# Layer two of a two-layer graph attention kernel: later rounds for some stages, and one wait for the row gathers of a round

## The chip, the cores and the metric

The kernel runs on one core of a Trainium2 chip. The metric is the device time of one execution in microseconds (us); lower is better. The kernel before takes 2671.73 us, the median of three runs (2668.62 to 2673.74).

Five engines of the core matter here. TensorE (PE) multiplies matrices and transposes tiles; its weight loads are listed apart (PEld). VectorE (DVE) and ScalarE (ACT) do elementwise work and reductions. GpSimd (POOL) does little here but issue indirect transfers, which fetch rows of a table by an index for each partition. SyncE (SP) issues the plain transfers. Each engine goes through its instructions in order; between engines they wait for each other by semaphores. The DMA engines carry out the transfers.

## The reference, cut to what matters

Two graph convolutions with attention, over 6250 nodes and 106,250 edges (50,000 in both directions and a loop at each node), the edges sorted by destination. There are 128 features in two heads of 64; an edge has 64 given attributes and 32 cosines of a time difference.

```python
def _transformer_conv(h, edge_attr, src, dst, Wq, bq, Wk, bk, Wv, bv, We, Ws, bs):
    q = (h @ Wq + bq).reshape(n, H, C)
    k = (h @ Wk + bk).reshape(n, H, C)
    v = (h @ Wv + bv).reshape(n, H, C)
    e = (edge_attr @ We).reshape(-1, H, C)
    alpha = einsum('ehc,ehc->eh', q[dst], k[src] + e) / sqrt(C)
    ex = exp(alpha - segment_max(alpha, dst)[dst])
    a = ex / segment_sum(ex, dst)[dst]
    out = segment_sum((v[src] + e) * a[:, :, None], dst)
    return out.reshape(n, H * C) + h @ Ws + bs

rel_t_enc = cos((node_vec[src] - edge_weight)[:, None] * time_w + time_b)
edge_attr = concatenate([rel_t_enc, edge_attr_64], axis=-1)
h = _transformer_conv(x, edge_attr, src, dst, ...)        # layer one
h = relu((h - mean(h, 0)) / sqrt(var(h, 0) + 1e-5) * bn_g + bn_b)
h = _transformer_conv(h, edge_attr, src, dst, ...)        # layer two
return layernorm(x + h)
```

## The kernel before

**Tiling.** The edges are cut into NC = 104 chunks of 1024 (`CE`), eight tiles (`T`) of 128 edges each. As the edges are sorted by destination, a chunk touches a window of at most NN = 64 nodes, which is handled as NQ = 4 groups of 16 nodes; each group takes part in three edge tiles (`window`, L693), one of them possibly from the chunk before. Both layers run through `conv(c, ...)` (L740), layer one with c = 0 and layer two with c = 1, one round for each chunk and some more for the pipeline. Layer two takes about the second half of the span, from some 1400 us on. No scheduler reorders the instructions (`tc.manual_schedule()`): each engine gets them in the order in which the program writes them, and waits are put in where data ask for them.

**What happens to a chunk in layer two**, with the tiles that the profile names:

- `fetch` (L768), SyncE: loads the edge attributes into the feature tile `ff`, the tables of the window (`ftab`, one transfer for each group), the cosines of layer one (`fz`), the turned attributes (`fet`), and the residual rows (`fr`).
- `gather` (L810), GpSimd: eight indirect transfers (L815), each of 128 rows of the hidden features, from `hn_d` to `ff`. They are issued three rounds ahead of the scores (`lead`, L824).
- `turn_in` (L876), TensorE: two times four transposes of the gathered rows into `fpx` (L885); ScalarE copies them to `fft` (L889).
- `score` (L900), TensorE: about 20 matmuls of the tables with `fft` and `fet` into `fps` (L916).
- `lowest` (L921), VectorE: the row minimum of the scores (L924) and a limit (L926); `weigh` (L928), ScalarE: the exponential (L931) into `fs`.
- `turn_weights` (L933), TensorE: three transposes of `fs` (L940) into `fppt`; ScalarE copies them to `fpt` (L941).
- `gather_sums` (L944), TensorE: 24 matmuls (L956) of `fpt` with `ff`, which sum weighted rows, attributes and weights for each node and head into the PSUM tile `fpa`.
- `divide` (L960), VectorE: divides these sums by the sums of weights (L963 to L966) into `fa`, and makes a 0/1 matrix `fsel` (L968).
- `finish_turn` (L976), TensorE: two joins (L978, L979; two instructions each in the profile), matmuls with `fsel` that turn `fa` and put its rows in place; VectorE copies the result to `fat` (L981).
- `product` (L984), TensorE: the closing products with the value weights and the edge weights (L993, L994, eight instructions in the profile) into PSUM.
- `complete` (L1000): VectorE adds the residual rows and takes away the mean (L1032 to L1034), ScalarE squares (L1036); for every second chunk come a square root with its table load (L1039), a reload of the table of the exponential (L1042) and a reciprocal. `store` (L1047), ScalarE: scales the rows; SyncE writes them out a little later (`send`).
- `attributes` (L1141 in the loop): VectorE copies the cosines `fz` into `ff`.

**The round loop** (L1059 to L1149) handles in round k chunk k+3 (fetched and gathered), k+1 (turned in), k (scores, lowest, weigh), k-1 (turned weights, sums), k-2 (divide, joins) and k-3 (products, complete). The order on TensorE is: scores of k, products of k-3, turned weights of k-1, joins of k-2, first half of the turning in of k+1, second half, extra work, sums of k-1. The extra work (`hide`, `pull`) is, in the first rounds, the writing of normalised rows to `hn_d`, and later up to four matmuls of the layer's tables (`tables`, L625) at a time, with some of the residual.

**Holds of GpSimd.** `bring` (L1068) issues the gathers one by one and ties each to a step of TensorE in the same round, so that they keep pace with it: the first to the end of the previous round's sums (`ended`), the second to the fourth score group (`half`), the third to the turned weights, the fourth to the joins, the fifth and sixth to the two halves of the turning in, the seventh and eighth to the fourth and the eighth of the 24 sums. Such a tie (`tc.add_manual_dep`, L819) is a wait on GpSimd.

**Buffers.** PSUM has eight banks: four for `fpx`, `fppt` and the extra work (`p_tr`), two for the scores (`p_s`), two for `fpa` (`p_a`). A bank of `p_a` belongs to one chunk: its first half holds the sums (`s.pa`), its second half the joins (`s.po`), and the products go into the place of the first join. In SBUF layer two has six feature tiles `ff` (L744: `bufs=6 if c else AHEAD + 3`, with AHEAD = 4) and seven of `fr` (L806).

**The last rounds.** `SWITCH` is NC - 3 = 101. From there on `finish` (product and complete) of k-2 takes the place of product and complete of k-3, and behind the loop the last chunks are written out stage by stage (L1148 to L1189). For the first RAW = 6 chunks the rows come from layer one's raw output `h_d`, and `normalise` (L970) is applied to them on VectorE.

Of the kernel before, what the change touches and what calls it, by code (L numbers as in the profile page):

```python
# [10 lines left out]
OP = mybir.AluOpType  # L11
# [53 lines left out]
SWITCH = NC - 3  # L65
STARTS = (*range(0, NC - 2, LG), NC - 2, NC - 1)
# [599 lines left out]
def ordered(ctx: ExitStack, tc: tile.TileContext, pl, x, dst, edge_attr_64, conv2, bn_g, bn_b, out):  # L666
# [73 lines left out]
    def conv(c, extra, first_blocks=None):  # L740
# [27 lines left out]
        def fetch(k):  # L768
# [9 lines left out]
            s.f = f = load.tile([P, T, FW], F32, name="ff")  # L778
# [22 lines left out]
            if c:  # L801
# [4 lines left out]
                s.r = load.tile([NN, D], F32, name="fr", bufs=7)  # L806
# [137 lines left out]
        def gather_sums(k):  # L944
# [3 lines left out]
            s.po = bank[:, 1].rearrange("p (i n) -> p i n", i=2)  # L948
# [35 lines left out]
        def product(k):  # L984
            po, at = ch[k].po, ch[k].at
            if c == 0:
                nc.tensor.matmul(po[:, 0], wv[c], at[:, 0], start=True, stop=False)
                nc.tensor.matmul(po[:, 0], web[c], at[:, 1], start=False, stop=True)
                return
            at = at.rearrange("p i (n h) -> p i n h", h=H)  # L990
            for h in range(H):
                r = slice(h * C, (h + 1) * C)
                nc.tensor.matmul(po[:NN, 0, r], at[:, 0, :, h], wv[c][:, r], start=True, stop=False)  # L993
                nc.tensor.matmul(po[:NN, 0, r], at[:, 1, :, h], web[c][:, r], start=False, stop=True)  # L994
# [5 lines left out]
        def complete(k):  # L1000
            s = ch.pop(k)
            po = s.po
            if c == 0:

                res = small.tile([P, NN], F32, name="fres")
                heads = po[:, 0].rearrange("p (n h) -> p n h", h=H)
# [25 lines left out]
            nc.vector.scalar_tensor_tensor(res, po[:NN, 0], 1.0, s.r, op0=OP.mult, op1=OP.add, accum_out=mean)  # L1032
# [25 lines left out]

        with cs, tc.manual_schedule():  # L1059
            ended = None  # L1060
            for k in range(-lead(-NC), NC - 2 if c else NC + 3):
                def on(j):
                    return 0 <= j < NC

# [25 lines left out]
                if on(k - 3) and k <= SWITCH:  # L1090
                    product(k - 3)
# [11 lines left out]
                if on(k - 3) and k <= SWITCH:  # L1103
# [30 lines left out]
                if on(k - 2) and k >= SWITCH:  # L1134
# [3 lines left out]
                if c and on(k):  # L1138
                    if k < RAW:
                        normalise(k)  # L1140
                    nc.vector.tensor_copy(ch[k].f[:, :, 1 + D:1 + D + TD], ch[k].z)  # L1141
# [6 lines left out]
            if c:  # L1148
                last = NC - 1  # L1149

                def attributes(k):
                    nc.vector.tensor_copy(ch[k].f[:, :, 1 + D:1 + D + TD], ch[k].z)
# [407 lines left out]
```

## Time and profile before

| | before |
|---|---|
| median of 3 runs | 2671.73 us |
| profiled execution, own time | 2670.95 us |
| its span | 2669.1 us |
| mean granted TensorE clock | 0.879 |
| HBM traffic over the span | 141 GB/s |
| stretch 1460 to 2580 us (layer two): PE busy | 785.88 us of 1120 |
| the same: DVE, ACT, POOL busy | 331.08, 398.83, 698.15 us |
| the same: clock, DMA share | 0.87, 0.56 |

All times in the profile are of one execution. A line of the timeline has the start in us, the duration in us, the engine, the line of the program, the operation, the written and read tiles with their shapes, and the count of equal instructions that were drawn together; in square brackets stands the idle time of the engine ahead of it and what ended that idle time ("issue" is time in which no wait that the profile shows held the engine, "remote" a semaphore whose sender the profile does not name). A line of the groups has the sum and the mean of the busy time of all such instructions, and, behind the bar's second place, the idle time of the engine just before them with its releasers. A line of the waits has the engine, the line that waited, the releaser, the idle time in us, how often, and the longest one.

Busy time on an engine is not the same as being the limit: a wait can move from one engine to another, and an engine's idle time costs nothing where another one sets the round.

### The profile page before, as it was taken

To read this page: it belongs to the slowest core of one execution; us is meant where nothing else is said; L and a number is where in the kernel's file an instruction comes from. 1 tells how busy PE (TensorE), PEld (TensorE's weight loads), DVE (VectorE), ACT (ScalarE), POOL (GpSimd) and SP (SyncE) were. 2 spreads that over 40 slices of the span, in tenths; PEclk is the share of its full clock that TensorE was granted. 3 is DMA by queue.
4 is the path that set the end of the run, shared out by engine and by line. 5 is a ranking of instruction groups with operands and counts; after the bars stand their busy time and mean duration, and the time that the engine had idled before them with its cause. 6 is when DMAs were issued, how large, how long until landed. Compare 5 with 4: busy or idle time off the path is not lost. (4 is left out here: it accounts for less than half of the span.)

```text
span 2669.1 us, 50291 instructions
## 1 busy us (share of the span) xinstructions
PE 1851.4 (69%) x14961; PEld 1107.9 (42%) x14961; DVE 1148.0 (43%) x3998; ACT 1082.5 (41%) x1906; POOL 1588.3 (60%) x1684
## 2 busy tenths in 40 slices
PE   3677767777777677677746667676767767676666
PEld 2444444444444444444424334444444434443443
DVE  3555555555555555565625222333232322232223
ACT  1455545553434444454532333333333333333333
POOL 4466666666666666666345666666666666666662
PEclk8799889988989989889977888888888898888888
DMA  6455555555555555555447555555555555555542
GB/s 177 128 148 146 146 153 145 144 143 151 146 147 138 152 148 145 144 144 138 126 118 194 148 140 148 152 153 147 143 150 148 157 147 142 154 143 140 128 134 52
DMA packets 535244, 383.29 MB, mean 144 GB/s; under 512 B 405638, under 2 KB 479258, under 8 KB 531634
## 3 DMA queue, kind: packets, MB, share of 16 engines
q1 hardware_dynamic: 460998, 231.66, 33.4%
q0 software_dynamic: 53184, 109.45, 17.1%
q10 hardware_dynamic: 20780, 38.87, 3.9%
q8 instruction: 122, 2.00, 0.3%
q14 instruction: 160, 1.31, 0.2%
HBM read 267.85 MB, written 108.49 MB: 141 GB/s over the span
## 5 line engine op out<-in xcount | busy, mean ns | idle before, releaser
L815 POOL DMA_INDIRECT ff<-xv_d,fsrcs x831 | 795.1, 957 | 511.2 <-issue 166.2
L815 POOL DMA_INDIRECT ff<-hn_d,fsrcs x783 | 743.6, 950 | 453.3 <-issue 172.3
L941 ACT COPY fpt<-fppt 128x384 f32<-128x384 f32 x208 | 99.6, 479 | 1261.9 <-PE fpx L885 705.6
L916 PE MATMUL fps<-fft,ftab 128*32 128x384 f32 (+2 forms) x2080 | 406.2, 498 | 146.5 <-issue 64.5
L956 PE MATMUL fpa<-ff,fpt 128*32 128x225 f32 x5008 | 350.6, 419 | 120.0 <-DVE fres L1032 102.2
L924 DVE TENSOR_REDUCE flow<-fps 128x1 f32<-128x384 f32 x208 | 116.1, 558 | 587.6 <-PE fpx L885 352.7
L885 PE MATMUL fpx<-fident,ff 128*128 128x128 f32 x1664 | 276.9, 299 | 38.5 <-issue 25.8
L956 PEld LDWEIGHTS fpa<-ff,fpt 128*32 128x32 f32 x5008 | 167.6, 125 | 321.0 <-issue 233.7
L916 PEld LDWEIGHTS fps<-fft,ftab 128*32 128x32 f32 x2080 | 142.7, 124 | 323.6 <-issue 161.8
L894 PE MATMUL fpe<-fident,ff 128*112 128x128 f32 x832 | 142.4, 295 | 189.0 <-issue 184.3
L889 ACT COPY fft<-fpx 128x512 f32<-128x512 f32 x404 | 232.2, 575 | 45.7 <-remote 20.1
L885 PEld LDWEIGHTS fpx<-fident,ff 128*128 128x128 f32 x1664 | 221.0, 156 | 54.5 <-issue 36.1
L916 PE MATMUL fps<-fxT,ftab 112*32 112x384 f32 (+2 forms) x1040 | 218.4, 509 | 17.2 <-issue 16.8
L963 DVE TENSOR_SCALAR finv<-fpa 128x1 f32<-128x1 f32 x208 | 32.0, 154 | 446.8 <-PE fps L916 237.6
L916 PE MATMUL fps<-fet,ftab 112*32 112x384 f32 (+2 forms) x1040 | 167.4, 448 | 33.0 <-issue 32.7
L894 PEld LDWEIGHTS fpe<-fident,ff 128*112 128x112 f32 x832 | 97.1, 141 | 218.6 <-issue 213.1
L978 PE MATMUL fpa<-fsel,fa 128*128 128x128 f32 x416 | 103.3, 332 | 81.5 <-DVE fsel L968 46.5
L860 DVE SCALAR_TENSOR_TENSOR farg<-fturns,farg 128x256 f32<-128x256 f32 x312 | 132.9, 426 | 10.7
L895 ACT COPY fet<-fpe 112x512 f32<-112x512 f32 x208 | 124.6, 599 | 9.9 <-PE fps L916 2.8
L940 PE MATMUL fppt<-fident,fs 128*128 128x128 f32 x626 | 117.1, 296 | 13.4 <-issue 5.8
L931 ACT ACTIVATE fs<-fps,fm 128x384 f32<-128x384 f32 x208 | 120.5, 579 | 9.7 <-DVE fm L926 6.1
L867 ACT ACT_TABLE_LOAD x82 | 105.2, 1283 | 42.2 <-issue 34.7
(224 smaller groups left out, 2654.4 us busy)
## 6 DMA issues: line engine op xcount, KB each, us to landing
ff<-in_edge_attr SPq DMA_DIRECT2D x206, 256.0 KB
et_d<-fet SPq DMA_DIRECT2D x104, 448.0 KB
fxT<-et_d SPq DMA_DIRECT2D x104, 448.0 KB
tab_d<-fo ACTq DMA_DIRECT2D x26, 1024.0 KB
ftab<-tab_d SPq DMA_DIRECT2D x832, 32.0 KB
enc_d<-fzs SPq DMA_DIRECT2D x104, 128.0 KB
fz<-enc_d SPq DMA_DIRECT2D x104, 128.0 KB
ff<-xv_d,fsrcs POOLq DMA_INDIRECT x831
```

What stands on the lines that cost most here:

```text
L815: row = nc.gpsimd.indirect_dma_start(out=f[:, t, (1 if c else 0):1 + D], out_offset=None, in_=(h_d[:N, :] if k < RAW else hn_d) if c else ...
L860: nc.vector.scalar_tensor_tensor(arg, turn, -part, arg, op0=OP.mult, op1=OP.add)
L867: nc.scalar.activation(z[:, :len(of)], arg[:, :len(of)], AF.Sin, bias=qpi)
L885: last = nc.tensor.transpose(px[:, t * P:(t + 1) * P], s.f[:, u * 4 + t, 1:1 + D], ident)
L889: nc.scalar.copy(s.ft[:, u * GE:(u + 1) * GE], px)
L894: last = nc.tensor.transpose(pe[:EC, t * P:(t + 1) * P], s.f[:, u * 4 + t, 1 + D:], ident)
L895: nc.scalar.copy(s.et[:, u * GE:(u + 1) * GE], pe[:EC])
L916: steps.append(nc.tensor.matmul(s.ps[r, to:to + n], s.tab[:kd, r, i], (of.et if i else of.ft)[:kd, at:at + n], start=i == 0, stop=i == 1))
L924: nc.vector.tensor_reduce(low, s.ps, AX.X, OP.min)
L931: nc.scalar.activation(s.s[:, :s.ps.shape[1]], s.ps, AF.Exp, bias=s.bias, scale=-1.0)
L940: last = nc.tensor.transpose(pp[:, t * P:(t + 1) * P], s.s[:, t * P:(t + 1) * P], ident)
L956: steps.append(nc.tensor.matmul(s.pa[r], s.pt[:, t * P + g * GH:t * P + (g + 1) * GH], f[:, i % T, 1:1 + D + EW], start=t == 0, stop=t == ...
```

## The change

Rounds 0 to STEADY = NC - 8 = 96 of layer two are no longer handled by the loop's body but by a function of their own, `steady`. In round k it handles chunk k+3 (fetch, gather), k+1 (turning in), k (scores), k-1 (lowest, weigh, turned weights), k-2 (sums), k-3 (divide, joins), k-4 (products) and k-5 (complete). Lowest and weigh thus come a round behind the scores, the sums two rounds behind them, the joins three, the products four. The order on TensorE is: sums of k-2, scores of k, products of k-4, extra work, turned weights of k-1, joins of k-3, turning in of k+1.

The eight gathers of a round are issued in one go, and only the first is tied to a step: the last transpose of the turning in of the round before (`held`).

After round 96, `catch_up` brings the pipeline to where the loop's body expects it: `lowest` and `weigh` of chunk 96, `complete` of 92, `finish` of 93, divide, joins and `finish` of 94, sums of 95. Rounds 97 to 101 and the tail behind the loop run as before, with `finish(k - 2)` in each round of layer two.

In PSUM, layer two has one bank of `p_a` in place of two, and one fixed bank `fpo` (`joined`), of which the joins take the first half and the products a quarter of their own. `ff` gets seven buffers in place of six, `fr` nine in place of seven. Layer one keeps its order.

```diff
+STEADY = NC - 8
...
-        p_a = cs.enter_context(tc.tile_pool(name=f"fp_a{c}", bufs=2, space=bass.MemoryType.PSUM))
+        p_a = cs.enter_context(tc.tile_pool(name=f"fp_a{c}", bufs=1 if c else 2, space=bass.MemoryType.PSUM))
+        p_o = cs.enter_context(tc.tile_pool(name="fp_o", bufs=1, space=bass.MemoryType.PSUM)) if c else None
...
+        joined = p_o.tile([P, 4, P], F32, name="fpo") if c else None
...
-            s.f = f = load.tile([P, T, FW], F32, name="ff")
+            s.f = f = load.tile([P, T, FW], F32, name="ff", bufs=AHEAD + 3)
...
-                s.r = load.tile([NN, D], F32, name="fr", bufs=7)
+                s.r = load.tile([NN, D], F32, name="fr", bufs=9)
...
-            s.po = bank[:, 1].rearrange("p (i n) -> p i n", i=2)
+            s.po = joined[:, :2] if c else bank[:, 1].rearrange("p (i n) -> p i n", i=2)
+            s.product = joined[:NN, 2] if c else s.po[:, 0]
...
-                nc.tensor.matmul(po[:NN, 0, r], at[:, 0, :, h], wv[c][:, r], start=True, stop=False)
-                nc.tensor.matmul(po[:NN, 0, r], at[:, 1, :, h], web[c][:, r], start=False, stop=True)
+                nc.tensor.matmul(ch[k].product[:, r], at[:, 0, :, h], wv[c][:, r], start=True, stop=False)
+                nc.tensor.matmul(ch[k].product[:, r], at[:, 1, :, h], web[c][:, r], start=False, stop=True)
...
-            nc.vector.scalar_tensor_tensor(res, po[:NN, 0], 1.0, s.r, op0=OP.mult, op1=OP.add, accum_out=mean)
+            nc.vector.scalar_tensor_tensor(res, s.product, 1.0, s.r, op0=OP.mult, op1=OP.add, accum_out=mean)
...
+        def attributes(k):
+            nc.vector.tensor_copy(ch[k].f[:, :, 1 + D:1 + D + TD], ch[k].z)
+
+        def steady(k, held):
...
+            fetch(k + lead(k))
+            gather(k + lead(k), range(T), held)
+            if on(k - 1):
+                lowest(k - 1)
+            if on(k - 3):
+                divide(k - 3)
+            if on(k - 1):
+                weigh(k - 1)
+            if on(k - 5):
+                complete(k - 5)
+            if on(k - 2):
+                gather_sums(k - 2)
+            score(k)
+            if on(k - 4):
+                product(k - 4)
+            at_round[0] = k
+            if hidden:
+                hide(4 if k == 0 else 3)
+            else:
+                pull(extra, (3 if k == 3 else 2) if k < 6 else 1)
+            if on(k - 1):
+                turn_weights(k - 1)
+            if on(k - 3):
+                finish_turn(k - 3)
+            turn_in(k + 1, 0)
+            held = turn_in(k + 1, 1)
+            if k < RAW:
+                normalise(k)
+            attributes(k)
+            if done:
+                store(*done.pop(0))
+            return held
+
+        def catch_up(k):
+            lowest(k)
+            weigh(k)
+            for j in (k - 4, k - 3, k - 2):
+                while done:
+                    store(*done.pop(0))
+                if j == k - 2:
+                    divide(j)
+                    finish_turn(j)
+                (complete if j == k - 4 else finish)(j)
+            gather_sums(k - 1)
...
-            ended = None
+            ended = held = None
             for k in range(-lead(-NC), NC - 2 if c else NC + 3):
...
+                if c and 0 <= k <= STEADY:
+                    held = steady(k, held)
+                    if k == STEADY:
+                        catch_up(k)
+                    continue
...
-                if on(k - 3) and k <= SWITCH:
+                if not c and on(k - 3) and k <= SWITCH:
                     product(k - 3)
...
-                if on(k - 3) and k <= SWITCH:
+                if not c and on(k - 3) and k <= SWITCH:
                     complete(k - 3)
...
-                if on(k - 2) and k >= SWITCH:
+                if on(k - 2) and (c or k >= SWITCH):
                     finish(k - 2)
```

More of the change, by code (lines that the diff above doesn't have):

```diff
@@ L984, in product @@
         def product(k):
-            po, at = ch[k].po, ch[k].at
+            at = ch[k].at
             if c == 0:
-                nc.tensor.matmul(po[:, 0], wv[c], at[:, 0], start=True, stop=False)
-                nc.tensor.matmul(po[:, 0], web[c], at[:, 1], start=False, stop=True)
+                nc.tensor.matmul(ch[k].product, wv[c], at[:, 0], start=True, stop=False)
+                nc.tensor.matmul(ch[k].product, web[c], at[:, 1], start=False, stop=True)
                 return
```

9 lines of the change are left out of this document (4 added, 5 removed).

## The prediction

> **What bounds layer two now.** I read the busy shares first, then the GpSimd group and its waits in a steady stretch of layer two (1700 to 2600 us), then the timeline of a few rounds.
>
> ```profile
> PE 1851.4 (69%) x14961; PEld 1107.9 (42%) x14961; DVE 1148.0 (43%) x3998; ACT 1082.5 (41%) x1906; POOL 1588.3 (60%) x1684
> ```
> ```profile
> L815 POOL DMA_INDIRECT ff<-hn_d,fsrcs x593 | 561.1, 946 | 339.6 <-issue 131.1 <-PE fps L916 73.2 <-remote 46.4
> ```
> ```profile
> POOL ff L815 <- issue: 131.1, 422, 2.1
> ```
>
> No engine is full on average. 593 row gathers, eight a round, are 74.1 rounds in 900 us: **12.14 us a round**. A gather takes 0.946 us, and 422 of them follow the one before after 131.1/422 = 0.31 us, so back to back they come every 1.25 us. The other 171 gathers (2.3 a round) waited for another engine, (339.6 - 131.1)/171 = 1.22 us each. A round on GpSimd is 8 x 0.946 + 5.7 x 0.31 + 2.3 x 1.22 = 12.14 us: it is either gathering or held, and the holds are 2.8 us of it. Held by what? By TensorE steps, and the timeline shows when those become known:
>
> ```profile
> 2545.81 0.94 POOL L815 DMA_INDIRECT ff<-hn_d,fsrcs  x1 [1.21 <-PE fpx L885]
> 2546.53 1.35 PE L956 MATMUL fpa<-ff,fpt 128*32 128x225 f32 x24 [1.70 <-DVE fres L1032]
> ...
> 2552.06 0.94 POOL L815 DMA_INDIRECT ff<-hn_d,fsrcs  x1 [0.30 <-issue]
> ...
> 2554.37 0.16 DVE L963 TENSOR_SCALAR finv<-fpa 128x1 f32<-128x1 f32 x1 [4.81 <-PE fps L916]
> ...
> 2554.60 0.94 POOL L815 DMA_INDIRECT ff<-hn_d,fsrcs  x1 [1.60 <-PE fps L916]
> ```
>
> The 24 sum matmuls of a chunk (L956) end at 2547.88 by the trace. VectorE, which has been waiting for them, starts only at 2554.37: after a run of six gathers has stopped at 2553.00, and 1.37 us after that. I read this as: while GpSimd gathers without a break, TensorE's "done" hardly reaches anybody, and it comes in one burst some time F after GpSimd stops. The same happens after seven gathers:
>
> ```profile
> 2201.28 0.95 POOL L815 DMA_INDIRECT ff<-hn_d,fsrcs  x1 [0.30 <-issue]
> ...
> 2204.12 0.56 DVE L924 TENSOR_REDUCE flow<-fps 128x1 f32<-128x384 f32 x1 [2.17 <-remote]
> 2204.23 0.94 POOL L815 DMA_INDIRECT ff<-hn_d,fsrcs  x1 [2.00 <-remote]
> ```
>
> There F is 2204.12 - 2202.23 = 1.89 us. So a round has two or three pauses because gathers wait for steps whose news needs a pause.
>
> **The change.** The order of TensorE over a cycle stays: sums, scores, closing products, turned weights, joins, turning in. Only the chunk numbers move (joins k-3 for k-2, products k-4 for k-3), and the pulled extra work goes ahead of the turned weights. What differs is who waits inside a round. The eight gathers of a chunk now wait once, for the last transpose of the round before.
>
> *GpSimd.* One hold for 2.3. The eight gathers run for 7 x 1.25 + 0.946 = 9.70 us. Round = 9.70 + F + R + 0.15, where R is what TensorE has still to do, at the burst, up to the last transpose, and 0.15 is about the step from a release to the gather behind it (2204.12 to 2204.23 above is 0.11). It breaks even at F + R = 12.14 - 9.85 = 2.29 us.
>
> *F.* Not seen for a run of exactly eight: 1.37 after six, 1.89 after seven; below, 0.84 is the least I saw (GpSimd stopped at 2544.60, and VectorE's L924 went at 2545.44). I take 1.7, nearer the long run, and keep 0.84 and 1.9.
>
> ```profile
> 2543.66 0.94 POOL L815 DMA_INDIRECT ff<-hn_d,fsrcs  x1 [0.30 <-issue]
> ...
> 2545.44 0.56 DVE L924 TENSOR_REDUCE flow<-fps 128x1 f32<-128x384 f32 x1 [3.28 <-PE fpx L885]
> ```
>
> *R* decides. TensorE issues 67 matmul instructions in a plain round (24 sums, 20 scores, 8 products, 3 turned weights, 4 joins, 8 turned in). The trace holds one passage that is nearly the new regime: nine gathers without a break and a TensorE whose inputs were nearly all there.
>
> ```profile
> 2045.22 1.35 PE L956 MATMUL fpa<-ff,fpt 128*32 128x225 f32 x24
> 2046.39 1.47 PE L916 MATMUL fps<-fft,ftab 128*32 128x128 f32 x6
> ...
> 2049.32 0.28 PE L994 MATMUL fpa<-fwe,fat 128*64 128x64 f32 x2
> 2049.98 0.53 PE L940 MATMUL fppt<-fident,fs 128*128 128x128 f32 x3 [0.38 <-issue]
> 2051.40 0.40 PE L978 MATMUL fpa<-fsel,fa 128*128 128x128 f32 x2 [0.90 <-issue]
> 2052.86 1.07 PE L979 MATMUL fpa<-fsel,fa 128*128 128x128 f32 x2 [1.06 <-issue]
> 2054.29 0.66 PE L885 MATMUL fpx<-fident,ff 128*128 128x128 f32 x2 [0.36 <-PE fpa L979]
> 2056.01 0.37 PE L885 MATMUL fpx<-fident,ff 128*128 128x128 f32 x1 [1.06 <-issue]
> 2056.72 0.37 PE L885 MATMUL fpx<-fident,ff 128*128 128x128 f32 x1 [0.34 <-issue]
> ```
> ```profile
> 2045.72 1.06 POOL L815 DMA_INDIRECT ff<-hn_d,fsrcs  x1 [2.21 <-PE fpx L885]
> ...
> 2055.83 0.94 POOL L815 DMA_INDIRECT ff<-hn_d,fsrcs  x1 [0.30 <-issue]
> ```
>
> The first 52 instructions go in four microseconds; after that TensorE crawls, one or two instructions every 0.7 to 1.4 us, with idle put down to "issue", not to a semaphore. (Joins waited for VectorE's L963 to L968 there, which the change moves a round ahead; the crawl before and after them remains.) Eleven microseconds after the run's start, when an eight-gather run would have had its burst, four transposes were started and four left. In the new order TensorE starts later: sums need the copied weights (0.48 us of ScalarE) and, with one sum bank for two, L963 to L966 of the chunk before, behind these on VectorE:
>
> ```profile
> 2545.58 0.48 ACT L941 COPY fpt<-fppt 128x384 f32<-128x384 f32 x1 [9.22 <-PE fpx L885]
> ...
> 2554.76 0.45 DVE L966 TENSOR_SCALAR fa<-fpa,finv 128x225 f32<-128x225 f32 x1
> ...
> 2556.02 0.56 DVE L924 TENSOR_REDUCE flow<-fps 128x1 f32<-128x384 f32 x1 [0.42 <-PE fppt L940]
> ...
> 2558.21 0.41 DVE L981 COPY fat<-fpa 128x256 f32<-128x256 f32 x1
> ...
> 2558.54 0.30 DVE L1141 COPY ff<-fz 128x256 f32<-128x256 f32 x1
> ```
>
> That is 0.41 + 0.30 + 0.56 + 0.45 and four or five small ones of about 0.16 (as L963 above): 2.3 us from the burst to the first sum, less R itself, which passes on TensorE meanwhile: some 1 us after GpSimd starts again, where the passage above began 0.5 us before it. Those 1.5 us cost two or three crawling instructions, so about seven remain, of which each takes 0.13 to 0.2 us (eight transposes in 1.04 or 1.60 us):
>
> ```profile
> 2556.20 1.04 PE L885 MATMUL fpx<-fident,ff 128*128 128x128 f32 x8
> ...
> 2543.23 1.60 PE L885 MATMUL fpx<-fident,ff 128*128 128x128 f32 x8
> ```
>
> R = 7 x 0.165 = 1.2 us. Ends: 0, if the crawl lets all through (fewer steps now have a waiter), and 2.4, all of the last 15 instructions at the slow pace.
>
> [...]
>
> *Round:* 9.70 + 1.7 + 1.2 + 0.15 = 12.75 us, 0.61 more than 12.14. There are 97 steady rounds: **+59 us**.
>
> *ScalarE and the square-root chain* (L1036 to L1049) leave the place between turned weights and turned-in features. I count that as nothing: it shortens waits of TensorE ahead of scores, which the hold hides; without the hold it would be worth up to a table load of 1.28 us, twice, in every second round.
>
> ```profile
> 2547.33 1.28 ACT L1039 ACT_TABLE_LOAD   x1
> ```
>
> *Buffers* (seven feature tiles for six, nine residual rows for seven, one bank for joins and products): no instruction more, the readers are rounds back; nothing. *DMA:* the same transfers; gathers still land two rounds ahead of their transposes; nothing, or a part of F if bursts of eight delay SyncE's loads.
>
> *Catching up* after round 96 puts two closings, one division and a join in a row, with TensorE waiting for VectorE: two chains of about 2 us by the rows above, once, less what the later rounds then no longer do: +3 us (0 to 8). *Rounds 97 to 101* keep the old holds: nothing.
>
> ```profile
> span 2669.1 us, 50291 instructions
> ```
>
> **Sum.** The profiled execution took 2670.95 us (span 2669.1), the median of the runs is 2671.73, 0.8 above: 2671.7 + 59 + 3 = **2733 us**.
>
> **Rivals.**
>
> *TensorE gets through* (R near 0). For it: around one slow gather at 1463 the whole TensorE round took 6.6 us from 1462.93, so the work as such fits twice into the run of gathers:
>
> ```profile
> 1463.44 2.12 POOL L815 DMA_INDIRECT ff<-hn_d,fsrcs  x1 [0.31 <-issue]
> ```
> ```profile
> 1462.93 1.35 PE L956 MATMUL fpa<-ff,fpt 128*32 128x225 f32 x24 [2.47 <-DVE fres L1032]
> ...
> 1468.50 1.04 PE L885 MATMUL fpx<-fident,ff 128*128 128x128 f32 x8
> ```
>
> Against it: there the gather took 2.12 us, so GpSimd paused. Then the round is 9.85 + F: 11.05 (F 1.2) to 11.55 (F 1.7), -106 to -57 us; with the catching up about **2590 us**. This is the other side: one hold of 1.2 to 1.7 us in place of 2.8 us of holds. It decides where F + R falls under 2.29.
>
> *The crawl bites harder.* Extra matmuls of the tables (up to eight a round until about round 90) come on top, and the crawl starts before the products: 12 or more left at the slow pace, R = 2.4, F = 1.9: 14.15 us, +195 us, 2870; halfway to the forecast, about **2830 us**. For it: the passage above had no such extras.
>
> *TensorE is really full and the order is the same, so nothing happens*: 12.1 us stay, **2673 us**. [...] The starts speak against it: at 1462.93 the same round's work began and ended inside 6.6 us.
>
> **Chances.** Forecast (2675 to 2790) 0.49; gets through 0.27; harder crawl 0.18; no effect 0.06. The two slow cases and the forecast's slow part make slower 0.67. I count within 0.2%, some 5 us, as no change, about what runs of this kernel can tell apart. The range that leaves about one in ten out on each side is 2600 to 2850; the forecast's own is 2675 to 2790.
>
> **What would show it.** In the changed profile: GpSimd in runs of eight at 1.25 us with one pause a round (right in any case but "nothing happens"); the pause over 2.3 us, with transposes L885 being issued in it, and "issue" idle ahead of L940, L978 and L885 (the forecast), or under 1.8 us with L885 done before GpSimd stops (the first rival). L963 should no longer stand between sums and joins. I am wrong in kind if TensorE's "done" reaches VectorE during the gathers, or if transposes wait for gathers that have not landed.

## The result, and the profile after

| | before | changed |
|---|---|---|
| median | 2670.57 us (4 runs, 2668.62 to 2673.74) | 2909.91 us (4 runs, 2899.8 to 2912.81) |
| ratio, 95% interval | | 1.0889 (1.0870 to 1.0908) |
| profiled execution: own time, span | 2670.95, 2669.1 us | 2908.79, 2907.0 us |
| row gathers from 1700 to 2600 us | 593, a round of 12.14 us | 494, a round of 900 x 8 / 494 = 14.57 us |
| granted clock in that stretch | 0.87 | 0.72 |

The change costs 239 us; 97 rounds x (14.57 - 12.14) would be 236 of them, if every round were like those of this stretch. By the gathers themselves, the 94 rounds from the first gather of hidden features to the 752nd take 1358.8 us against 1142.3, which is 216 us more; from there to the end it is 104.4 us against 91.5. The forecast was 2733 us, the range 2600 to 2850: the sign was right, the size was not, and the time lies outside the range.

In the experiments the kernel before took 2668 to 2708 us at some times (**condition A**, to which the result above and the profiles of before and after belong) and 2203 to 2212 us at others (**condition B**), steadily within each, and chip 12 showed both, so each experiment is compared only with the kernel before as it ran on the same chip in the same session.

The groups of GpSimd and its waits, in the changed kernel from 1700 to 2600 us (count, busy us, mean ns of one, idle us before them with releasers; then idle us, times, longest):

```profile
L818 POOL DMA_INDIRECT ff<-hn_d,fsrcs x494 | 466.2, 944 | 435.9 <-PE fpx L888 295.1 <-issue 128.0 <-PE fpa L960 6.6
```
```profile
POOL ff L818 <- PE fpx L888: 295.1, 60, 7.0
...
PEld fppt L943 <- issue: 106.9, 130, 1.9
...
PE fpo L998 <- issue: 72.7, 94, 1.8
...
PE fpa L960 <- DVE fa L970: 29.9, 41, 2.4
```

There is one hold a round now, for the transposes (L888, L885 before), and it is 295.1 / 60 = 4.92 us long, in place of 2.3 holds of 1.22 us. TensorE's idle time is again put down to "issue": no wait that the profile shows holds it. Of the 311 gaps of that kind ahead of a matmul in the stretch (over 0.3 us of idle time, over 0.45 us from the start before), 248 stand ahead of one that waits for no semaphore at all. I say below that TensorE is *starved*: it has work whose inputs are there, and yet finds next to nothing to start. One round of the timeline (start, duration, engine, line, operation, tiles, count, idle time before and its releaser):

```profile
2110.21 0.94 POOL L818 DMA_INDIRECT ff<-hn_d,fsrcs  x1 [4.87 <-PE fpx L888]
...
2110.58 1.35 PE L960 MATMUL fpa<-ff,fpt 128*32 128x225 f32 x24 [0.64 <-ACT fft L892]
...
2113.20 0.32 PE L997 MATMUL fpo<-fwv,fat 128*64 128x64 f32 x2
...
2113.91 0.22 PE L998 MATMUL fpo<-fwe,fat 128*64 128x64 f32 x1 [0.39 <-issue]
...
2117.49 0.35 PE L998 MATMUL fpo<-fwe,fat 128*64 128x64 f32 x1 [1.11 <-issue]
...
2118.89 1.86 PE L631 MATMUL fpg<-fhT,fm 128*128 128x512 f32 x2 [1.05 <-issue]
2118.95 0.95 POOL L818 DMA_INDIRECT ff<-hn_d,fsrcs  x1 [0.30 <-issue]
...
2121.74 0.47 PE L943 MATMUL fppt<-fident,fs 128*128 128x128 f32 x1 [0.23 <-issue]
...
2122.01 0.64 PE L982 MATMUL fpo<-fsel,fa 128*128 128x128 f32 x2
...
2122.86 1.27 PE L888 MATMUL fpx<-fident,ff 128*128 128x128 f32 x8
...
2124.41 0.94 POOL L818 DMA_INDIRECT ff<-hn_d,fsrcs  x1 [4.51 <-PE fpx L888]
```

Sums and scores, 44 matmuls, go in three microseconds from 2110.58. Then, from 2113.2, one or two matmuls start every 0.7 to 1.4 us, though a product lasts only 0.2 to 0.35 (the "crawl" of the prediction): eight products, two matmuls of the tables and the first two turned weights take 8.5 us. GpSimd stops at 2119.90; from 2121.74 TensorE runs freely again, and still has joins and transposes to do before GpSimd may go on. Counted from the first of the sums over all rounds of the stretch, the first gap of over 0.45 us from start to start comes after 43 to 51 matmuls in 51 of 62 rounds (after 52 to 66 in the others), while the time that these took goes from 2.7 us (a tenth of the rounds is below) to 4.6 us (a tenth is above). In twelve rounds the first 40 took 4.15 us or more, at the slow pace of TensorE, and in eleven of these the gap comes after 44 or 46; in 22 they took 2.15 us or less, and in 15 of these it comes after 43 to 49. So it looks like a stock of matmuls, which the pause fills up, rather than a stock of time.

### The profile page after: what moved, and what is told of

Same layout as the page of the kernel before. It is cut to its first block, busy times and chain, and to the rows that moved or that the text cites. A ratio compares the mean times of both kernels' runs of the same rounds, so it can differ in the third digit from the quotient of the medians.

```text
span 2907.0 us, 49641 instructions
## 1 busy us (share of the span) xinstructions
PE 1918.3 (66%) x14961; PEld 1219.3 (42%) x14961; DVE 1127.1 (39%) x3998; ACT 1093.3 (38%) x1906; POOL 1583.5 (54%) x1684
## 4 chain that ended last, share of the span: by engine, by line
PE 26%; issue 15%; DVE 6%; another core or an unknown queue 2%; ACT 1%; DVEq 0%; DMA 0%; POOL 0%; SPq 0%; ACTq 0%; POOLq 0%
PE fpa L960 6%; PE fps L919 5%; PE fppt L943 3%; PE fpg L631 3%; PE fpo L997 2%; PE fpo L998 2%; PE fpo L982 2%; PE fpo L983 1%; DVE flow L927 1%; PE fpx L888 1%; DVE fa L970 1%; PE fpg L1358 1%; DVE ff L1063 1%; ACT fft L892 1%
## 5 line engine op out<-in xcount | busy, mean ns | idle before, releaser
L960 PE MATMUL fpa<-ff,fpt 128*32 128x225 f32 x5008 | 389.4, 457 | 108.8 <-DVE fa L970 60.9
L888 PE MATMUL fpx<-fident,ff 128*128 128x128 f32 x1664 | 323.4, 337 | 58.8 <-issue 34.1
L919 PE MATMUL fps<-fft,ftab 128*32 128x384 f32 (+2 forms) x2080 | 322.8, 501 | 54.0 <-issue 36.3
L888 PEld LDWEIGHTS fpx<-fident,ff 128*128 128x128 f32 x1664 | 265.5, 180 | 76.1 <-issue 44.2
L985 DVE COPY fat<-fpo 128x256 f32<-128x256 f32 x104 | 43.9, 422 | 617.0 <-PE fpo L983 576.9
L943 PEld LDWEIGHTS fppt<-fident,fs 128*128 128x128 f32 x626 | 88.1, 160 | 182.1 <-issue 178.0
L919 PE MATMUL fps<-fxT,ftab 112*32 112x384 f32 (+2 forms) x1040 | 152.7, 481 | 1.4 <-issue 1.4
L639 DVE SCALAR_TENSOR_TENSOR fo<-fpg,fb,fcode 128x512 f32<-128x512 f32 x50 | 57.1, 1146 | 245.3 <-PE fpg L631 114.5
L998 PE MATMUL fpo<-fwe,fat 128*64 128x64 f32 x416 | 76.7, 241 | 110.2 <-issue 109.7
L637 ACT ACTIVATE fo<-fpg,fb 128x512 f32<-128x512 f32 x50 | 59.3, 1190 | 200.3 <-PE fpg L631 110.3
```

Of the source, the lines that this page charges most:

```text
L888: last = nc.tensor.transpose(px[:, t * P:(t + 1) * P], s.f[:, u * 4 + t, 1:1 + D], ident)
L919: steps.append(nc.tensor.matmul(s.ps[r, to:to + n], s.tab[:kd, r, i], (of.et if i else of.ft)[:kd, at:at + n], start=i == 0, stop=i == 1))
L943: last = nc.tensor.transpose(pp[:, t * P:(t + 1) * P], s.s[:, t * P:(t + 1) * P], ident)
L960: steps.append(nc.tensor.matmul(s.pa[r], s.pt[:, t * P + g * GH:t * P + (g + 1) * GH], f[:, i % T, 1:1 + D + EW], start=t == 0, stop=t == ...
L998: nc.tensor.matmul(ch[k].product[:, r], at[:, 1, :, h], web[c][:, r], start=False, stop=True)
```

## The experiments

### Which part of the change costs

Two kernels separate it: the shifted rounds with the eight old holds, and the rounds of before with the one new hold.

```diff
-            gather(k + lead(k), range(T), held)
+            j = k + lead(k)
...
-                gather_sums(k - 2)
+            sums = gather_sums(k - 2) if on(k - 2) else (None,) * 3
+            for t, step in enumerate(sums):
+                gather(j, (t,), step)
+            half, _ = score(k)
+            gather(j, (3,), half)
...
+            gather(j, (4,), turn_weights(k - 1) if on(k - 1) else None)
+            gather(j, (5,), finish_turn(k - 3) if on(k - 3) else None)
+            gather(j, (6,), turn_in(k + 1, 0))
+            gather(j, (7,), turn_in(k + 1, 1))
```

> The shifted rounds and the new buffers stay, but the gathers of a round are tied one by one to eight steps again (three among the sums, one each to the fourth score group, the turned weights, the joins and the two halves of the turning in). Theory 'starved TensorE': behind a stock of about 47 matmuls, TensorE gets an instruction only every 0.7 us or so while GpSimd gathers without a break, so the time is set by how often GpSimd pauses; with the old pauses the round comes back to 12.1 us, 2640 to 2710 us in all. Rival 'long chain': the shift itself costs, since with one bank for the sums VectorE's chain (L985, L1063, L927, L967 to L970) now stands between joins and sums whatever GpSimd does; the round stays near 14.5 us, 2850 to 2910 us.

```diff
-        load = cs.enter_context(tc.tile_pool(name=f"fload{c}", bufs=6 if c else AHEAD + 3))
+        load = cs.enter_context(tc.tile_pool(name=f"fload{c}", bufs=AHEAD + 3))
...
+                single = c and 0 <= k <= NC - 8
...
+                elif single:
+                    bring(range(T), held)
...
-                step = turn_in(k + 1, 1) if on(k + 1) else None
+                step = held = turn_in(k + 1, 1) if on(k + 1) else None
```

> The kernel before with its own rounds and its two sum banks, but with the eight gathers of rounds 0 to 96 tied once, to the last transpose of the round before (and seven feature buffers). Theory 'starved TensorE': one pause a round, so the round is 14 to 14.6 us as in the changed kernel, 2850 to 2910 us. Rival 'long chain': the hold alone is harmless, 2640 to 2710 us.

Both fell into condition B: 2207.51 us for the shift (ratio 1.0014, 1.0003 to 1.0025) and 2204.16 us for the hold, with the kernel before at 2204.78 us. Neither range was met, since the kernel before itself took 466 us less; what had been asked stayed open. The same two on a second chip, again in B, took 2210.39 and 2202.5 us against 2208.8. On a third chip, condition A came up:

> The shifted rounds with eight holds, on a third chip. Where the kernel before takes 2205 us: 2205 us. Where it takes 2670 us, theory 'starved TensorE': 2640 to 2710 us; rival 'the new order costs, not the hold': 2850 to 2910 us.

> The kernel before with one hold a round, on a third chip. Where the kernel before takes 2205 us: 2205 us. Where it takes 2670 us, theory 'starved TensorE': 2850 to 2910 us; rival 'the new order costs, not the hold': 2670 us.

Here the kernel before took 2703.6 us, the shift with old holds 2715.92 (1.005 of it, one run, 6 us above its range), the one hold alone 2867.16 (1.060, one run, inside its range). The groups of GpSimd from 1700 to 2600 us, of the shift and of the one hold:

```profile
L818 POOL DMA_INDIRECT ff<-hn_d,fsrcs x581 | 548.0, 943 | 351.6 <-remote 125.7 <-issue 119.5 <-PE fpx L888 44.5
```
```profile
L815 POOL DMA_INDIRECT ff<-hn_d,fsrcs x516 | 489.3, 948 | 411.1 <-PE fpx L885 268.7 <-issue 135.3 <-PE fpg L1302 4.6
```

581 gathers are a round of 12.39 us, 516 one of 13.95. The hold alone thus costs 164 us of the 239, the rounds alone 12. Together they give 14.57 us (in another session), so that some 60 us come only with both. A part of it may be seen in the waits of the changed kernel above: the sums wait for VectorE's L970 there, 29.9 us in 62 rounds, which the one sum bank asks for, and with one hold that delay, too, could be paid in it; no run separates it.

The hold can also be left out altogether (the first gather of a round waits for nothing but its buffer):

```diff
-            gather(k + lead(k), range(T), held)
+            gather(k + lead(k), range(T))
```

> The changed kernel without its hold: the gathers of rounds 0 to 96 wait for nothing but their buffers. On a chip where the kernel before takes 2205 us, the theory is that the gathers at 1.25 us are the only limit and the hold is met before GpSimd comes to it, so nothing changes: 0.997 to 1.003 of the kernel before. Rival: the hold and the buffers still cost a part of each round, 0.98 or less. On a chip where it takes 2670 us, theory 'starved TensorE': GpSimd pauses only when the feature buffers run out, TensorE crawls for longer, 2900 us or more; rival 'the pause of the hold is the cost': 2500 us or less.

In the same session it took 3040.84 us, 1.1244 (1.1211 to 1.1276) of the kernel before. So it isn't the waiting as such that costs. The timeline of GpSimd shows that it goes on until the buffers run out, and then waits longer (5.59 us, for sums):

```profile
2103.74 0.94 POOL L818 DMA_INDIRECT ff<-hn_d,fsrcs  x1 [0.30 <-issue]
2110.27 0.95 POOL L818 DMA_INDIRECT ff<-hn_d,fsrcs  x1 [5.59 <-PE fpa L960]
```

### The same two kernels in condition B

> The changed kernel itself, beside the kernel before on one chip. In the last group of runs the kernel before took 2205 us, not 2671, so TensorE's gaps depend on the chip as well. Theory 'starved TensorE depends on the chip': on a chip where the kernel before takes about 2205 us, the changed one has no gaps of 0.7 to 1.4 us behind 47 matmuls either, the gathers at 1.25 us set the round (8 x 1.25 = 10.0 us) and the ratio is 1.00 (0.995 to 1.005); on a chip where it takes 2670 us, the ratio is 1.09 again. Rival 'the change costs by itself': the ratio is 1.05 or more on either chip.

> The kernel before, for its trace on this chip. By the same theory, where it takes about 2205 us: VectorE's L963 goes within 1 us of the last sum, GpSimd has no pauses of over 1 us for TensorE's steps, and the round is 10 us; where it takes 2670 us, the trace is that of before. Rival: TensorE itself runs faster on that chip (transposes closer than 0.107 us, a granted clock well over 0.88), and GpSimd pauses as often.

The changed kernel took 2209.17 us and the kernel before 2208.77 (medians); the ratio over all runs is 0.9996 (0.9985 to 1.0007), no difference. The theory held, the rival did not. GpSimd's groups from 1300 to 2100 us, before and changed:

```profile
L815 POOL DMA_INDIRECT ff<-hn_d,fsrcs x638 | 606.5, 951 | 194.6 <-issue 71.1 <-PE fpx L885 35.7 <-DMA ff<-hn_d,fsrcs 30.5
```
```profile
L818 POOL DMA_INDIRECT ff<-hn_d,fsrcs x639 | 606.6, 949 | 195.0 <-issue 165.7 <-PE fpx L888 11.6 <-DMA ff<-hn_d,fsrcs 7.6
```

638 and 639 gathers in 800 us are 1.25 us each, 10.0 us a round: GpSimd has no pause left to lose. A gather takes as long as in A (949 against 944 ns). What differs is TensorE beside it; this is the timeline of the kernel before in B:

```profile
1704.92 1.35 PE L956 MATMUL fpa<-ff,fpt 128*32 128x225 f32 x24
...
1706.33 0.16 DVE L963 TENSOR_SCALAR finv<-fpa 128x1 f32<-128x1 f32 x1 [0.70 <-PE fpa L956]
```

VectorE's L963 goes 0.06 us after the last of the 24 sums ends, in the middle of a run of gathers; in A it went 6.5 us after, once GpSimd had paused. TensorE of the changed kernel, too, has no gaps put down to "issue" among its longest waits here: it waits for rows to land (187.4 us at L888 in 800).

### Is it the gathers that starve TensorE?

From round 12 to round 96, SyncE loads the first 1024 rows of the table in place of the gathers, as many bytes into the same places; GpSimd is idle, and the second layer's sums are those of other rows.

```diff
+            if k < 12:
+                gather(k + lead(k), range(T), held)
+            else:
+                for t in range(T):
+                    nc.sync.dma_start(ch[k + lead(k)].f[:, t, 1:1 + D], hn_d[t * P:(t + 1) * P, :])
```

> The changed kernel, but from round 12 to round 96 the rows of a chunk do not come by GpSimd's indirect transfers: SyncE loads the first 1024 rows of the table in eight plain transfers of the same 128 x 512 bytes, so the second layer's sums are those of other rows. GpSimd is idle there. Theory 'starved TensorE by GpSimd's gathers': the gaps of 0.7 to 1.4 us put down to issue ahead of L997, L998, L943 go, TensorE's round takes some 7 us, with VectorE's chain of 2.3 us a round is 9 to 10.5 us, 2450 to 2560 us in all. Rival 'TensorE is full': its own work sets the time, the round stays at 14 us or more, about 2900 us. Rival 'it is the traffic, not GpSimd': the same bytes move, the gaps stay, 2800 us or more.

> The changed kernel with SyncE's plain loads of the first 1024 rows in place of the gathers from round 12 to round 96 (the second layer's sums are those of other rows). It took 2388 us on a chip where the kernel before takes 2205 us. On a chip where that takes about 2700 us, theory 'starved by GpSimd's gathers': without them TensorE has no gaps, and the second layer runs as on the other kind of chip; only the first layer, some 270 us longer there, and twelve rounds keep the difference: 2640 to 2720 us, some 250 us less than the changed kernel. Rival 'starved whatever GpSimd does' (the traffic, or TensorE's instructions as such): the gaps ahead of L997, L998, L943 stay, 2850 us or more.

The first of these fell into B: 2387.66 us, 183 over the kernel before and below the range expected; as B has no gaps in any case it told nothing of them, only that the loads come late (the transposes wait 125.7 us for them from 1300 to 2200 us, and the sums 188.6 us for the copied weights). The second fell into A and is the experiment that decides: 2688.13 us, where the kernel before takes 2668.14, inside the range of the theory and some 160 us below that of the rival. Stretches of 900 us of the second layer, B and A (busy us and count of each engine, granted clock, DMA share, GB/s):

```profile
1300.00:2200.00 900.00, 555.34 (x5075) 359.04 (x5079) 245.65 (x1069) 320.32 (x682) 0.00 (x0) 0.77 0.55 146
```
```profile
1600.00:2500.00 900.00, 557.86 (x5046) 359.49 (x5046) 244.17 (x1066) 316.43 (x674) 0.00 (x0) 0.77 0.55 147
```

Without GpSimd's gathers the two conditions cannot be told apart here: the counts agree within 1.2%. The 300 us between the two runs lie elsewhere, 243 of them ahead of the first gather of hidden features (at 1432.7 us in A, 1189.7 in B) and most of the rest in the rounds that still gather. From the 72nd gather of hidden features to the 80th, between which the plain loads lie, it is 1047.4 us in A and 1033.2 in B. TensorE waits for rows and for copied weights there in both (121.5 and 189.6 us in A), so this kernel gains nothing on the one before. And this is TensorE in A without them:

```profile
2099.75 1.14 PE L960 MATMUL fpa<-ff,fpt 128*32 128x225 f32 x20
...
2102.52 0.28 PE L998 MATMUL fpo<-fwe,fat 128*64 128x64 f32 x2
...
2103.70 0.49 PE L943 MATMUL fppt<-fident,fs 128*128 128x128 f32 x3
...
2104.25 0.39 PE L983 MATMUL fpo<-fsel,fa 128*128 128x128 f32 x2
```

Sums to joins in 4.9 us, with no gap behind the scores. That the bytes moved, or TensorE's own work, made the gaps is refuted: as many bytes move in a round, and more in a microsecond (147 GB/s against 124 in the changed kernel), and the same matmuls run. In A it is GpSimd's gathering that starves TensorE; by which way, this run does not show.

One more rival is that TensorE's instructions are loaded late. The packets of the changed kernel in A, from 1700 to 2600 us, speak against it (queue, kind, packets, MB, share):

```profile
q8 instruction: 35, 0.57, 0.3%
```

That is one block of 16 KB every 15 to 31 us, or 35 blocks in 62 rounds, while every round has its gaps. A block takes 0.88 to 1.45 us, in B (44 blocks in 800 us) 0.89 to 1.49. The other instruction queue moves 38 packets in the same time. When a block was asked for, the packets don't tell.

### A stock of matmuls

The scores of rounds 0 to 96 are issued twice into the same bank (20 matmuls more).

```diff
             score(k)
+            score(k, ch[k].ps)
```

> The changed kernel with the score matmuls of rounds 0 to 96 issued twice, one after the other into the same bank (20 matmuls more in a round, the same result). Theory 'starved TensorE': on a chip where the kernel before takes 2670 us, TensorE has a stock of about 47 matmuls while GpSimd gathers, and beyond it each costs about 0.7 us; 20 more cost up to 14 us a round, at least 5 us, so 3400 us or more. Rival 'TensorE is slow only by its own work': the 20 cost their busy time of 1.1 to 1.7 us a round, 3000 to 3100 us. On a chip where the kernel before takes 2205 us no stock shows, the 20 fit beside the gathers (TensorE has 26% idle) or cost at most their busy time: 2205 to 2370 us.

> The changed kernel with the score matmuls issued twice, on another chip; on one where the kernel before takes 2205 us it took 2209 us. On a chip where that takes about 2700 us, theory 'stock of 47 matmuls': 20 more find the stock empty, each costs about 0.7 us while GpSimd gathers, and those left behind the run about 0.1 us; the crawl of a run (some 6 us) then takes in about 9 fewer of the late steps, so the pause grows by 2 to 4 us: 3100 to 3350 us. Rival 'a stock of time, not of instructions' (TensorE works for the first 3 us or so of a run, whatever the number): the 20 cost their busy time of 1.1 to 1.7 us, 3000 to 3080 us.

In B it cost nothing: 2209.23 us against 2208.8. In A it took 3202.0 us, where the kernel before takes 2707.76 (37 us more than where the changed kernel took 2910; the changed kernel was not run beside it). The hold grew from 4.92 us to 394.3 / 50 = 7.89:

```profile
POOL ff L818 <- PE fpx L888: 394.3, 50, 9.5
```

The rival's price for a stock of time (up to 3080 us) falls, with these 37 us, too; the first estimate of mine, 3400 or more, was too high, as it let none of the late steps be done in the pause. The timeline of TensorE in A:

```profile
2099.86 1.35 PE L960 MATMUL fpa<-ff,fpt 128*32 128x225 f32 x24 [1.35 <-DVE fa L970]
...
2101.67 0.82 PE L919 MATMUL fps<-fxT,ftab 112*32 112x384 f32 x8
...
2104.63 1.24 PE L919 MATMUL fps<-fft,ftab 128*32 128x384 f32 x3 [1.14 <-issue]
...
2107.52 0.48 PE L919 MATMUL fps<-fft,ftab 128*32 128x384 f32 x1 [0.90 <-issue]
```

The gaps now fall into the second scores: the first one comes after 43 to 51 matmuls in 50 of 51 rounds, now in 2.2 to 3.5 us. The place moved to other instructions, the number stayed. This run alone does not tell a number from a time, since the first gap comes at much the same time behind the first gather, too; what tells them apart are the rounds at the slow pace above.

### Feeding TensorE by a second pause

```diff
-            gather(k + lead(k), range(T), held)
+            gather(j, range(4), held)
...
                 product(k - 4)
+            gather(j, range(4, T), ch[k - 4].last if on(k - 4) else None)
```

> The changed kernel with a second hold: gathers one to four are tied to the last transpose of the round before, gathers five to eight to the last closing product of the same round. Theory 'starved TensorE': two pauses of about 1.5 us instead of one of 4.9 us; the products, turned weights, joins and transposes then no longer crawl; the round is 12 to 13.3 us, 2660 to 2780 us. Rival 'long chain': a second hold adds a wait and takes none away, 2900 us or more.

> The changed kernel with two holds: gathers one to four behind the last transpose of the round before, five to eight behind the last closing product. On a chip where the kernel before takes about 2700 us, theory 'starved TensorE': a pause after four gathers lets TensorE take up new instructions, round 12 to 13.3 us, 2690 to 2810 us, clearly under the one-hold kernel's 2867 to 2910 us. Rival 'each hold costs a pause of its own': 2950 us or more. On a chip where it takes 2205 us: 2205 us.

In B 2207.04 us, 1.0007 (0.9996 to 1.0018). In A 2803.82 us against 2668.14, a ratio of 1.051 in one run: less than one hold costs (1.060 without the shift, 1.089 with it), at the upper end of the range, and still slower than the old holds. GpSimd's waits from 1700 to 2600 us in A:

```profile
POOL ff L818 <- PE fpo L998: 208.6, 57, 4.8
```

The hold for the products is 3.7 us on average, not 1.5: by then the stock is used up, and TensorE has to wait until GpSimd has been still for a while before it can finish them. From there it runs through joins and transposes, and the other hold mostly costs nothing (3.3 us in the stretch). The stock is no fixed number either: with two holds the first gap comes after 33 to 41 matmuls from the first of the sums in 65 of 67 rounds; the pause lies elsewhere there.

### Wider spacing

Two memsets of 128 x 40 on GpSimd behind each gather, to see whether the gathers starve TensorE only when they come at 1.25 us.

```diff
-            gather(k + lead(k), range(T), held)
+            for t in range(T):
+                gather(k + lead(k), (t,), None if t else held)
+                nc.gpsimd.memset(spin, 0.0)
+                nc.gpsimd.memset(spin, 0.0)
```

> The changed kernel with two small memsets of GpSimd (128 x 40, about 0.13 us each) behind each gather, so that gathers come every 1.5 to 1.6 us instead of every 1.25. On a chip where the kernel before takes about 2700 us, theory 'backlog': a run of gathers leaves something behind GpSimd that takes longer than 1.25 us for each (the 12.14 us of the kernel before over eight are 1.52 us), and TensorE gets its instructions again only when that is worked off; at this spacing there is little backlog, TensorE is done within the run, the round is 12.3 to 13.5 us, 2690 to 2810 us. Rival 'any gathering starves TensorE, at whatever pace': a pause of 4 us or more stays on top of a run of 12 us, 16 us a round, 3050 us or more. On a chip where it takes 2205 us: the gathers set the round, 12 to 13.2 us, 2400 to 2520 us.

> The kernel with spaced gathers once more, on another chip. Where the kernel before takes about 2700 us, theory 'backlog': 2690 to 2810 us. Rival 'any gathering starves TensorE, at whatever pace': 3050 us or more. Where it takes 2205 us: 2405 us again.

All three runs (2405.08 and, on chip 12, 2405.49 and 2404.51 us, with the kernel before at 2211, 2203 and 2205) fell into B. There the gathers and memsets set the round, 12.1 us at this spacing, as expected. For A nothing is known: the question stays open.

## Why the prediction was wrong

**What bounds it.** Right, and now shown for A: GpSimd's gathers and pauses set the round, and TensorE gets on freely only in the pauses and for some 47 matmuls behind them. The reading "TensorE's 'done' hardly reaches anybody" was one half of it. The other half, that TensorE itself gets nothing to start once its stock is used up, stood in the text as the crawl. TensorE is not full: without gathers its round is done in 4.9 us and eight transposes.

**Run of gathers, 9.70 us.** Right: 8 x 0.944 and 7 x 0.305 are 9.69.

**F, 1.7 us.** Right: from GpSimd's stop to the last stretch of TensorE without gaps it is 1.85 us on average over 59 pauses (a tenth of them under 1.67, a tenth over 2.26). That is taken where TensorE starts again; the prediction took F where VectorE hears of it.

**R, 1.2 us and 0.15 to the release.** This is the step that failed: what TensorE still has to do when GpSimd has stopped was priced too low. R and the release measured 3.1 us over the same 59 pauses, where I had 1.35 and bounds of 0.15 to 2.55; 1.75 us over 97 rounds are 170 of the 177 us by which the forecast was short. It has three parts. First the count: I had seven instructions left, and on average twelve stand in the last stretch alone, which are four joins and eight transposes; in 53 of the 62 pauses none of these twelve starts before GpSimd stops. I had taken the count from a passage without table matmuls, where TensorE had begun ahead of GpSimd; in the changed kernel the 62 rounds hold 71 of L631, mostly in pairs, with 30.7 us of idle time ahead of them, and 72 of the residual in eights, with 8.5 us. Second the pace: I took the mean of two, 0.165 us; in the pauses the median from transpose to transpose is 0.213 us. The windows of one microsecond show why (the last but two columns are the granted clock, DMA share and GB/s):

```profile
2112.00:2113.00 1.00, 1.00 (x19) 0.52 (x11) 0.00 (x0) 0.00 (x0) 0.69 (x2) 1.00 0.22 64
2113.00:2114.00 1.00, 0.61 (x7) 0.26 (x3) 0.00 (x0) 0.00 (x0) 0.70 (x2) 1.00 0.29 72
...
2116.00:2117.00 1.00, 0.32 (x2) 0.20 (x2) 0.00 (x0) 0.00 (x0) 0.70 (x2) 0.75 1.06 246
...
2122.00:2123.00 1.00, 1.00 (x6) 1.00 (x6) 0.00 (x0) 0.98 (x2) 0.00 (x0) 0.50 0.91 220
2123.00:2124.00 1.00, 1.00 (x9) 0.90 (x7) 0.89 (x4) 0.77 (x3) 0.00 (x0) 0.83 0.83 303
```

TensorE's work thins out at 2113.5, the clock falls to half within 2116, some 3 us later, and is back only when the last transposes run. In the trace of the changed kernel the clock stays full or half for 3.41 us or a multiple of it at a time (339 of its 340 stretches), and TensorE is not idle ahead of a fall: in the 3.41 us ahead of the 61 falls from 1700 to 2600 us that follow the first gap of a round, it was busy for 35% of the time in the median (23 to 48% in eight of ten), ahead of the 62 rises for 92% (85 to 100%). From transpose to transpose the median in this stretch is 0.213 us at half clock and 0.109 us at full. Third the tail: from the start of the last transpose (2109.64 by its group of eight) to the gather (2110.21) it is 0.57 us, not 0.15, with the transpose's own 0.30 us in it.

With these terms the sum comes out: 9.69 + 1.85 + 11 x 0.21 + 0.57 = 14.4 us, against 14.57 measured.

The upper bound of R was also added up wrongly. "All of the last 15 instructions at the slow pace" of 0.2 us are 3.0 us, not 2.4; with them the round would have been 9.70 + 1.7 + 3.0 + 0.15 = 14.55 us and the time about 2908 us, close to the result. Two smaller slips: VectorE's rows between burst and sums add up to 2.4 to 2.5 us, not 2.3, and halfway between 2870 and 2733 is 2801, not 2830. The start of TensorE's round was not the fault: its sums begin 0.6 us behind the first gather on average, where I had 1 us.

**Catching up, +3 us (0 to 8).** Too low: GpSimd stands for 15.78 us there, 10.9 more than in another round, once, and the whole of the end is 12.9 us longer than before.

```profile
2820.55 0.94 POOL L818 DMA_INDIRECT ff<-hn_d,fsrcs  x1 [15.78 <-PE fps L919]
```

**ScalarE's chain, buffers, transfers at nothing.** Nearly right: the shift with the old holds, which has all of them and the catching up, costs 12 us in A.

**The rivals.** "The crawl bites harder" was what happened. Its own sum was 14.15 us a round and 2870 us; I moved it towards the forecast, to 2830, gave it 0.18, and let the range end at 2850. Its argument (extra matmuls come on top, the passage had none) was a fact of the changed kernel's rounds and belonged in the forecast. "TensorE gets through" is what B looks like (2209 us, no loss, but also no gain, as the gathers at 1.25 us are the floor). "TensorE is full" is refuted by the plain loads.

**What no row could show.** All of this holds in condition A. In B the change does nothing at all. The trace of before shows the starving in plain sight, and I took it for a property of the kernel.

## What to carry to other kernels

A wait that costs time can still be what feeds another engine: before several holds are drawn together into one, look at what happens on the held engine's neighbours during the pauses, and count how many of their instructions a pause must cover. When an engine's idle time has no releaser ("issue"), count the instructions from the last free stretch to the first gap; if the number stays the same while the time does not, it may be a stock, and instructions that are added ahead of the critical one can make the wait longer, as the doubled scores did here. And what a kernel is tuned to depends on the condition that it is tuned in: holds that are worth 6% in A are worth nothing in B.

## What the runs showed of the hardware

The same program takes 2203 to 2212 or 2668 to 2708 us, depending on the time at which it runs and not on the chip alone, with the same gathers (0.95 us, every 1.25 us) and the same matmuls. In the second layer the difference goes with GpSimd's gathers: with plain loads in their place it has the same pace in both. The first layer, which gathers as well, is some 245 us longer in A (the first gather of hidden features comes at 1435.3 us against 1188.1); there no run took the gathers out.

The trace itself has a second sign, which is less clear. Counted from 1700 to 2600 us, 921 instructions of VectorE raise its semaphore in the kernel before (A), and the trace holds 322 of these events; with plain loads in A (1700 to 2500 us) it holds all 760 of 760; in B (before, 1300 to 2100 us) 940 of 992. In A, about 4.6 semaphore events a microsecond are recorded while GpSimd gathers and 11.9 while it pauses (pauses of over 0.32 us), in B 29.9 throughout. So in A events go missing while GpSimd gathers. But what is missing does not go with the time lost: in A the trace of the changed kernel holds 628 of 736, and that of the kernel with no hold, the slower of the two, 686 of 690. Matmuls are not missing beside them: the pages of both kernels have all 14961, in A and in B. Whether the missing events and the starving have to do with each other, or both come of a third thing, can't be told here: every run was recorded, and none without the recording was made. What brings condition A about was not found either.
